# Layer 0's attention matrix: a hand-set order of all engines up to it, with an early mask, four row buffers and split square pieces

## Chip, cores and metric

One NeuronCore of a Trainium2 chip. The metric is the device time of one execution in microseconds (us). The engines are named as in the profile: PE (matmuls), DVE (VectorE), ACT (ScalarE), POOL (GpSimd), SP (issues the transfers). All times inside a run are us from the start of its span. The granted clock is the share of PE's full clock that the chip allows; a spell below 1.00 is called a throttle here.

## The reference, cut

Four graph layers act on x, shaped 32 x 512 x 128, with one 512 x 512 matrix `adj`. The change concerns what comes before layer 0's first product: layer 0 needs the softmax of a matrix `A` that is built from `adj` and a vector `e`, its diagonal apart. Layer 1 needs `adj` and a polynomial of it (here `cheb`, twice adj squared less the identity).

```python
    def _L0_gnn_ref(input, adj, W, e, bias):
        NEG = -9000000000000000.0
        h0 = jnp.einsum('bnf,fg->bng', input, W[0])
        h1 = jnp.einsum('bnf,fg->bng', input, W[1])
        m = adj > 0
        idx = jnp.cumsum(m.reshape(-1).astype(jnp.int32)) - 1
        vals = e[0][idx].reshape(adj.shape)
        A = jnp.where(m, vals, jnp.float32(NEG))
        A = jax.nn.softmax(A, axis=1)
        M = jnp.eye(adj.shape[0], dtype=A.dtype)
        out = jnp.einsum('ij,bjg->big', A * M, h0) + jnp.einsum('ij,bjg->big', A * (1.0 - M), h1)
        return out + bias[None, None, :]
    ...
    h = jnp.maximum(_layernorm(x, axis=-1), 0.0)
    x = x + _L0_gnn_ref(h, adj, L0_gnn_W, L0_gnn_e, L0_gnn_bias)
    # layers 1, 2, 3 likewise, with other bodies
```

## The kernel before

The 32 batches go in 16 pairs. `adj` lies in four blocks of 128 rows (NT = 4). A part of the program, from the masks to the attention matrix, is in the order of the source on PE, DVE, ACT and POOL (`manual_schedule`); what follows is ordered by an automatic scheduler, which may also pull an operation forward into the hand-ordered part. An engine works through its own list in order, and this is what the case is about: in b_mask below, ACT stands idle for 2.80 us before a copy, although the exponential behind it has had its input since 36.54.

```python
    def cheb_rows(i):                       # one square piece: 4 f32 matmuls (8 records in the profile), 3.43 us of PE
        p = bank(f"p_cheb_{i}")
        for t in range(NT):
            nc.tensor.matmul(p, adjT[:, t, blk(i)], adj_s[:, t, :], start=(t == 0), stop=(t == NT - 1))
        nc.scalar.mul(cheb[:, i, :], p, 2.0)
        nc.gpsimd.tensor_sub(cheb[:, i, blk(i)], cheb[:, i, blk(i)], ident)
    # ... masks m, prefix counts, one-hot rows (at_row, at_col); cheb_rows(0), cheb_rows(1)
    def softmax_rows(t):
        ph, pv = scores[t]
        none = prep.tile([P, N], F32, tag="none", name=f"none_{t}", bufs=2)
        nc.gpsimd.tensor_scalar(none, m[:, t, :], -1.0, -NEG, OP.add, OP.mult)      # the mask
        u = prep.tile([P, N], F32, tag="u", name=f"u_{t}", bufs=2)                  # a row buffer
        nc.vector.scalar_tensor_tensor(u, ph, elastn, none, OP.mult, OP.add)
        nc.vector.tensor_add(u, pv, u)
        nc.vector.tensor_reduce(least[:, t : t + 1], u, axis=AX.X, op=OP.min)
        nc.scalar.activation(u, u, AF.Exp, bias=least[:, t : t + 1], scale=-1.0,
                             accum_out=total[:, t : t + 1])
        return u

    def scaled_rows(t, u):
        nc.vector.reciprocal(total[:, t : t + 1], total[:, t : t + 1])
        nc.scalar.mul(split(att[:, t, :]), crossed(u), total[:, t : t + 1])
        nc.vector.scalar_tensor_tensor(diag[:, t, :], u[:, blk(t)], total[:, t : t + 1], ident, OP.mult, OP.mult)
        own = split(att[:, t, :])[:, :, t, :]
        nc.vector.tensor_sub(own, own, diag[:, t, :].rearrange("p (b c) -> p b c", c=QR))

    score_rows(0)
    score_rows(1)
    u = softmax_rows(0)
    cheb_rows(2)
    score_rows(2)
    for t in range(1, NT):
        un = softmax_rows(t)
        scaled_rows(t - 1, u)
        u = un
        if t == 1:
            score_rows(3)
            next(first[1])                  # transposes of pair 1
            cheb_rows(3)
    scaled_rows(NT - 1, u)
    attT = square_tile("attT")
    transpose_square(att, attT, "attT")     # 16 transposes on PE, 4 copies
    for _ in sum_steps(attT, "att", nc.vector):
        pass
    # ... adiag; projection of pair 1; then layer 0, in automatic order
```

## Time and profile before

| | kernel before |
|---|---|
| median of the first three runs | 1012.33 us |
| span of the profiled run | 1010.4 us |
| PE busy | 974.9 us |
| PE idle | 35.5 us |
| start of layer 0's first product | 59.17 us |
| start of layer 1's first product | 219.8 us |

A profile line of a timeline gives start, duration, engine, source line, operation, the tile written and the tiles read, the count, and in square brackets how long the engine stood idle just before and what ended that. The lines that carry the argument are in the prediction.

### The profile page before, as it was taken

How to read it: one execution, taken by the hardware profiler on the slowest of the kernel's cores; microseconds unless marked ns; L12 is line 12 of the kernel's file. 1: busy time of each engine (PE TensorE's matmuls, PEld its weight loads, DVE VectorE, ACT ScalarE, POOL GpSimd, SP SyncE). 2: the span in 40 equal slices, each digit the busy share in tenths (PEclk: the TensorE clock that was granted, in tenths of full speed). 3: DMA queues.
4: the chain of work that ended last, by engine and by line, in shares of the span. 5: the costliest groups of instructions: out<-in, count | busy, mean ns of one | idle time of the engine just before them, and what ended most of it. 6: DMA issues, size and time to landing. Idle time of an engine off the chain costs nothing.

```text
span 1010.4 us, 16117 instructions
## 1 busy us (share of the span) xinstructions
PE 974.9 (96%) x5918; PEld 808.2 (80%) x5918; DVE 631.5 (63%) x1526; ACT 443.1 (44%) x968; POOL 390.6 (39%) x470
## 2 busy tenths in 40 slices
PE   7698999999999999999999999999999999999997
PEld 4298999999999999998877777778667677777775
DVE  7477887755656565556846888777764544444443
ACT  4474445413223232326656433333565544444553
POOL 1258998762124421315555322221133222233332
PEclk9899999999999999999989999999999999999999
DMA  9136644511312122123434333323232112121111
GB/s 250 47 110 171 178 121 133 147 52 55 84 42 67 60 64 63 47 79 91 118 84 114 116 103 103 95 77 85 63 85 73 53 55 72 53 73 43 53 33 42
DMA packets 83007, 87.17 MB, mean 86 GB/s; under 512 B 6768, under 2 KB 73072, under 8 KB 82928
## 3 DMA queue, kind: packets, MB, share of 16 engines
q1 hardware_dynamic: 82928, 86.14, 30.4%
q8 instruction: 47, 0.77, 0.3%
q14 instruction: 32, 0.26, 0.1%
HBM read 44.70 MB, written 41.42 MB: 85 GB/s over the span
## 4 chain that ended last, share of the span: by engine, by line
PE 89%; DVE 6%; ACT 2%; DMA 1%; issue 1%; POOL 1%; SPq 0%; POOLq 0%; DVEq 0%; ACTq 0%
PE p_av L713 11%; PE p_score L701 10%; PE p_l L343 10%; PE p_msgT_c L290 4%; PE p_x1T_c L290 4%; PE p_x2T_c L290 4%; PE p_l_c L297 4%; PE p_hv L343 3%; PE p_msgT_a L290 3%; PE p_x1T_a L290 3%; PE p_x2T_d L290 3%; PE p_x2T_a L290 3%; PE p_x1T_d L290 3%; PE p_qkh L688 3%; PE p_msgT_d L290 2%; PE p_g L343 2%
## 5 line engine op out<-in xcount | busy, mean ns | idle before, releaser
L209 ACT ACTIVATE h<-x,sh,rs 128x128 f32<-128x128 f32 x384 | 154.4, 482 | 61.1 <-PE p_x2T_d L290 45.5
L706 POOL TENSOR_TENSOR ex<-ex,adjTx 128x512 f32<-128x512 f32 x64 | 83.3, 1304 | 200.2 <-issue 147.7
L702 ACT ACTIVATE ex<-p_score 128x512 f32<-128x512 f32 x128 | 71.8, 587 | 130.8 <-issue 113.0
L713 PEld LDWEIGHTS p_av<-qkh_hv,ex 128*128 128x128 f32 x1024 | 118.7, 191 | 11.5 <-issue 6.9
L713 PE MATMUL p_av<-qkh_hv,ex 128*128 128x129 f32 x1024 | 121.2, 275 | 2.2 <-POOL ex L706 1.4
L701 PE MATMUL p_score<-qkh_hv,hT 128*128 128x512 f32 x256 | 115.2, 593 | 0.0
L236 DVE STREAM_TRANSPOSE hb_hT<-h 128x512 f32<-128x512 f32 x122 | 84.7, 700 | 24.6 <-ACT h L209 23.7
L190 DVE BATCH_NORM_STATS2 bn<-x 128x6 f32<-128x256 f32 x256 | 95.4, 421 | 2.0
L706 DVE TENSOR_TENSOR ex<-ex,adjTx 128x512 f32<-128x512 f32 x64 | 45.9, 717 | 75.7 <-ACT ex L704 75.7
L701 PEld LDWEIGHTS p_score<-qkh_hv,hT 128*128 128x128 f32 x256 | 46.3, 191 | 46.4 <-issue 44.4
L704 ACT ACTIVATE ex<-ex 128x512 f32<-128x512 f32 x128 | 76.5, 630 | 1.8
L268 POOL TENSOR_TENSOR rt_h<-h 128x256 f32<-128x256 f32 x16 | 11.6, 727 | 133.9 <-PE p_x2T_c L290 133.1
L268 POOL TENSOR_TENSOR rt_feat<-feat,feat 128x256 f32<-128x256 f32 x16 | 11.6, 726 | 126.4 <-ACT feat L660 126.4
L666 POOL TENSOR_TENSOR x<-x,phi2b 128x1024 f32<-128x1024 f32 x16 | 38.0, 2377 | 33.2 <-ACT h L209 33.2
L343 PE MATMUL p_l<-th,x1T 128*128 128x128 f32 x256 | 49.5, 275 | 0.0
L343 PE MATMUL p_l<-th,x2T 128*128 128x128 f32 x256 | 49.5, 275 | 0.0
L343 PE MATMUL p_l<-th,hs 128*128 128x128 f32 x256 | 49.5, 275 | 0.0
L343 PEld LDWEIGHTS p_hv<-vw,hT 128*128 128x128 f32 x256 | 33.6, 192 | 14.9 <-issue 7.9
L369 ACT COPY g<-p_g 128x512 f32<-128x512 f32 x32 | 18.3, 579 | 61.3 <-PE p_g L343 56.2
L570 POOL TENSOR_TENSOR hd<-hT,adiag 128x512 f32<-128x512 f32 x32 | 40.4, 1274 | 3.7 <-PE p_l_e L591 2.5
L673 ACT ACTIVATE h1T<-p_phi,phi1b 128x512 f32<-128x512 f32 x32 | 21.9, 685 | 44.9 <-PE p_phi L672 44.9
L343 PEld LDWEIGHTS p_l<-th,hs 128*128 128x128 f32 x256 | 40.1, 192 | 0.8
(223 smaller groups left out, 2179.6 us busy)
## 6 DMA issues: line engine op xcount, KB each, us to landing
d_hT<-hb_hT SPq DMA_DIRECT2D x244, 128.0 KB
hT<-d_hT SPq DMA_DIRECT2D x61, 512.0 KB
x<-in_x_dram SPq DMA_DIRECT2D x32, 256.0 KB
out_dram<-x SPq DMA_DIRECT2D x32, 256.0 KB
adj_s<-in_adj_dram SPq DMA_DIRECT2D x4, 256.0 KB
adjT_d<-adjT SPq DMA_DIRECT2D x1, 1024.0 KB
sq<-in_adj_dram SPq DMA_DIRECT2D x4, 256.0 KB
adjTx<-adjT_d SPq DMA_DIRECT2D x4, 256.0 KB
```

The costliest lines, as they stand in the source:

```text
L190: ins = nc.vector.bn_stats(st[:, k].rearrange("p e s -> p (e s)"), xt[q][:, b, t : t + 2, :].rearrange("p t f -> p f t"))
L209: nc.scalar.activation(h[:, b, t, :], xt[q][:, b, t, :], AF.Relu, bias=shift[q][:, i : i + 1], scale=scale[q][:, i : i + 1])
L236: nc.vector.transpose(hb[:, :, b].rearrange("p j t r -> p t j r"), h[:, b].rearrange("p t (j c) -> p t j c", c=QR))
L290: nc.tensor.matmul(p[:, :H], b[:, k, :], a[:, k, :], start=(first and k == 0), stop=(k == 1), skip_group_check=True)
L297: nc.tensor.matmul(p[:, i * D : (i + 1) * D], a[:, k, blk(i)], b[:, k, :], start=(first and i == 0 and k == 0), stop=(k == 1), skip_group_ ...
L343: nc.tensor.matmul(p[:, blk(t)], hT(t), w, start=(i == 0), stop=(i == len(terms) - 1))
L570: nc.gpsimd.tensor_mul(split(s), src, split(scale))
L701: nc.tensor.matmul(ps, hT[:, t, b, :], qkh, start=True, stop=True)
L702: nc.scalar.activation(ex[:, t, :], ps, AF.Tanh, scale=1.0 / (8.0 * math.sqrt(D)))
L704: nc.scalar.activation(ex[:, t, :], ex[:, t, :], AF.Exp, scale=8.0)
L706: eng.tensor_mul(ex[:, t, :], ex[:, t, :], adjTx[0][:, t, :])
L713: nc.tensor.matmul(po[:, i, : D + 1], ex[:, t, blk(i0 + i)], hv[:, t, :], start=(t == 0), stop=(t == NT - 1))
```

## The change

The intent: PE waits 10.3 us for the rows of the attention matrix. So the order of all four engines up to it is written anew. The mask is made as soon as `m` exists and put into `att` itself, all four rows have a buffer of their own, the diagonal goes from DVE to POOL, `adj` is transposed row by row, a square piece is split in halves that fit holes, pieces 2 and 3 move behind the softmax, the statistics and normalization of pairs 0 and 1 are spread over waits, and the sums for the seven-product scheme are ordered as the products use them.

```diff
+    att = square_tile("att")
+    for t in range(NT):
+        nc.gpsimd.tensor_scalar(att[:, t, :], m[:, t, :], -1.0, -NEG, OP.add, OP.mult)
+    pt = [bank(f"p_adjT_{j}") for j in range(NT)]
+    for t in range(NT):
+        transpose_rows(pt, adj_s, t)        # row t into four banks
...
     def softmax_rows(t):
         ph, pv = scores[t]
-        none = prep.tile([P, N], F32, tag="none", name=f"none_{t}", bufs=2)
-        nc.gpsimd.tensor_scalar(none, m[:, t, :], -1.0, -NEG, OP.add, OP.mult)
-        u = prep.tile([P, N], F32, tag="u", name=f"u_{t}", bufs=2)
-        nc.vector.scalar_tensor_tensor(u, ph, elastn, none, OP.mult, OP.add)
+        u = prep.tile([P, N], F32, tag="u", name=f"u_{t}", bufs=NT)
+        nc.vector.scalar_tensor_tensor(u, ph, elastn, att[:, t, :], OP.mult, OP.add)
...
-        nc.vector.scalar_tensor_tensor(diag[:, t, :], u[:, blk(t)], total[:, t : t + 1], ident, OP.mult, OP.mult)
         own = split(att[:, t, :])[:, :, t, :]
-        nc.vector.tensor_sub(own, own, diag[:, t, :].rearrange("p (b c) -> p b c", c=QR))
+        d = diag[:, t, :].rearrange("p (b c) -> p b c", c=QR)
+        nc.gpsimd.tensor_mul(d, own, ident.rearrange("p (b c) -> p b c", c=QR))
+        nc.gpsimd.tensor_sub(own, own, d)
...
+    for t in range(NT):
+        score_rows(t)
+    next(project[0])
...
+    for t in range(NT):
+        if t == NT - 1:
+            next(project[0], None)          # two copies on ACT
+        us.append(softmax_rows(t))
+        if t == 0:
+            next(ln[1], None)
+        else:
+            scaled_rows(t - 1, us[t - 1])
+        for _ in range(3):
+            next(normal[1], None)           # normalization of pair 1
+    scaled_rows(NT - 1, us[-1])
+    next(turned[1])                         # transposes of pair 1
+    for t in range(NT):
+        transpose_rows(pt, att, t)
+    next(turned[1], None)
...
+    next(project[1])
+    for q in (2, 3):
+        next(ln[q])                         # statistics of pairs 2 and 3
...                                         # copies of attT, sums, adiag
+    for i in (2, 3):
+        for _ in pieces[i]:                 # square pieces 2 and 3
+            pass
     by_source.__exit__(None, None, None)
...
-        for out, op, p, q in ((s3, OP.subtract, a11, a21), (a21, OP.add, a21, a22),
-                              (s2, OP.subtract, a21, a11), (s4, OP.subtract, a12, s2)):
+        for out, op, p, q in ((s1, OP.add, a21, a22), (s2, OP.subtract, s1, a11),
+                              (a21, OP.subtract, a11, a21), (s4, OP.subtract, a12, s2)):
```

More of the change, by code (lines that the diff above doesn't have):

```diff
@@ L184, in ln_stats, with stats_steps @@
     def ln_stats(q, hold=False):
+        for _ in stats_steps(q, hold):
+            pass
+    def stats_steps(q, hold=False):
         st = stats.tile([P, NT, 2, 3], F32, tag="bn", name=f"bn_{q}", bufs=4)
@@ L193, in ln_stats @@
                 tc.keep_in_program_order(ins)
+        yield
         sd = stats.tile([P, NT, 2], F32, tag="sd", name=f"sd_{q}", bufs=4)
         nc.scalar.activation(sd, st[:, :, :, 2], AF.Sqrt, bias=eps, scale=1.0 / D)
+        yield
         rs = stats.tile([P, NT, 2], F32, tag="rs", name=f"rs_{q}")
@@ L201, in ln_stats, with normed_tile, normed_steps @@
         scale[q] = rs.rearrange("p k e -> p (k e)")
-    def normed(q, on_act=True):
-        h = work.tile([P, 2, NT, D], F32, tag="h", name=f"h_{q}", bufs=3)
+    def normed_tile(q):
+        return work.tile([P, 2, NT, D], F32, tag="h", name=f"h_{q}", bufs=3)
+    def normed_steps(q, h):
         for b in range(2):
@@ L207, in normed @@
                 i = b * NT + t
-                if on_act:
-                    nc.scalar.activation(h[:, b, t, :], xt[q][:, b, t, :], AF.Relu,
-                                         bias=shift[q][:, i : i + 1], scale=scale[q][:, i : i + 1])
-                else:
-                    nc.vector.tensor_scalar(h[:, b, t, :], xt[q][:, b, t, :], scale[q][:, i : i + 1],
-                                            shift[q][:, i : i + 1], OP.mult, OP.add)
-            if not on_act:
-                nc.scalar.activation(h[:, b], h[:, b], AF.Relu)
+                nc.scalar.activation(h[:, b, t, :], xt[q][:, b, t, :], AF.Relu,
+                                     bias=shift[q][:, i : i + 1], scale=scale[q][:, i : i + 1])
+                yield
+    def normed(q, on_act=True):
+        h = normed_tile(q)
+        if on_act:
+            for _ in normed_steps(q, h):
+                pass
+            return h
+        for b in range(2):
+            for t in range(NT):
+                i = b * NT + t
+                nc.vector.tensor_scalar(h[:, b, t, :], xt[q][:, b, t, :], scale[q][:, i : i + 1],
+                                        shift[q][:, i : i + 1], OP.mult, OP.add)
+            nc.scalar.activation(h[:, b], h[:, b], AF.Relu)
         return h
@@ L223, in transposed_by_pe, with pe_steps @@
         hT = feature_major(name)
+        for _ in pe_steps(h, name, hT):
+            pass
+        return hT
+    def pe_steps(h, name, hT):
+        ps = [bank(f"p_{name}_{b}") for b in range(2)]
         for b in range(2):
-            p = bank(f"p_{name}_{b}")
             for t in range(NT):
-                nc.tensor.transpose(p[:, blk(t)], h[:, b, t, :], ident)
+                nc.tensor.transpose(ps[b][:, blk(t)], h[:, b, t, :], ident)
+        yield
+        for b, p in enumerate(ps):
             nc.scalar.copy(hT[:, :, b, :].rearrange("p b (a c) -> p b a c", c=QR), crossed(p))
-        return hT
     def transposed(h, name):
@@ L256, in sum_steps @@
         extra = const.tile([P, 3, 2, H], F32, tag="sums", name=f"sums_{name}", bufs=3)
-        s2, s3, s4 = extra[:, 0], extra[:, 1], extra[:, 2]
-        sums[name] = {1: a11, 2: a12, 3: s4, 4: a22, 5: a21, 6: s2, 7: s3}
-        for out, op, p, q in ((s3, OP.subtract, a11, a21), (a21, OP.add, a21, a22),
-                              (s2, OP.subtract, a21, a11), (s4, OP.subtract, a12, s2)):
+        s1, s2, s4 = extra[:, 0], extra[:, 1], extra[:, 2]
+        sums[name] = {1: a11, 2: a12, 3: s4, 4: a22, 5: s1, 6: s2, 7: a21}
+        for out, op, p, q in ((s1, OP.add, a21, a22), (s2, OP.subtract, s1, a11),
+                              (a21, OP.subtract, a11, a21), (s4, OP.subtract, a12, s2)):
             tc.keep_in_program_order(eng.tensor_tensor(out, p, q, op))
@@ L357, in layer0_first @@
     def layer0_first(q):
-        ln_stats(q, hold=q in (2, 3, 4))
-        yield
+        if q >= 4:
+            ln_stats(q)
+            yield
         h = normed(q)
@@ L365, in layer0_first, with project_steps, transpose_rows @@
             yield
+        for _ in project_steps(q, hT):
+            pass
+    def project_steps(q, hT):
         g = pair_tile(f"g_{q}").rearrange("p (t b f) -> p t b f", t=NT, b=2)
+        pg = [projected(f"p_g_{q}_{b}", (at(hT, b), w0[:, 1, :])) for b in range(2)]
+        yield
         for b in range(2):
-            pg = projected(f"p_g_{q}_{b}", (at(hT, b), w0[:, 1, :]))
-            nc.scalar.copy(g[:, :, b, :], pg)
+            nc.scalar.copy(g[:, :, b, :], pg[b])
         early[q] = hT, g
-    def transpose_square(src, dst, name):
+    def transpose_rows(banks, src, t):
         for j in range(NT):
-            p = bank(f"p_{name}_{j}")
-            for i in range(NT):
-                nc.tensor.transpose(p[:, blk(i)], src[:, i, blk(j)], ident)
-            nc.scalar.copy(dst[:, j, :], p)
+            nc.tensor.transpose(banks[j][:, blk(t)], src[:, t, blk(j)], ident)
     adjT = prep.tile([P, NT, N], F32, name="adjT")
@@ L385, in cheb_rows @@
         for t in range(NT):
+            if t == 2:
+                yield
             nc.tensor.matmul(p, adjT[:, t, blk(i)], adj_s[:, t, :], start=(t == 0), stop=(t == NT - 1))
+        yield
         nc.scalar.mul(cheb[:, i, :], p, 2.0)
         nc.gpsimd.tensor_sub(cheb[:, i, blk(i)], cheb[:, i, blk(i)], ident)
-    first = {q: layer0_first(q) for q in range(NQ)}
+    first = {q: layer0_first(q) for q in range(2, NQ)}
     m = prep.tile([P, NT, N], F16, name="m")
@@ L402 @@
     nc.vector.tensor_copy(rch, rc)
-    transpose_square(adj_s, adjT, "adjT")
+    att = square_tile("att")
[4 more added lines that the diff above has]
+        transpose_rows(pt, adj_s, t)
+    for j in range(NT):
+        nc.scalar.copy(adjT[:, j, :], pt[j])
     adjT_d = bounce.tile([N, N], F32, tag="adjT", name="adjT_d", bufs=1)
@@ L415 @@
                          start=(t == 0), stop=(t == NT - 1))
-    next(first[0])
-    next(first[0])
     incl = prep.tile([P, NT], F32, name="incl")
@@ L423 @@
     nc.vector.tensor_scalar(befh, before, float(NE), None, OP.min)
-    cheb_rows(0)
+    pieces = [cheb_rows(i) for i in range(NT)]
+    next(pieces[0])
     of_row = prep.tile([P, NT, NE], F16, name="of_row")
@@ L439 @@
                              start=(t == 0), stop=(t == NT - 1))
-    next(first[0])
+    next(pieces[0])
     row_of = prep.tile([P, NK], F32, name="row_of")
@@ L456 @@
                                 accum_out=row_of[:, kk : kk + 1])
+    ln = [stats_steps(q) for q in range(4)]
+    next(ln[0])
+    next(ln[0])
     bk = prep.tile([P, NK], F32, name="bk")
@@ L464 @@
                                 accum_out=col_of[:, kk : kk + 1])
+        next(ln[0], None)
+    h = {q: normed_tile(q) for q in range(2)}
+    hT = {q: feature_major(f"hT0_{q}") for q in range(2)}
+    normal = [normed_steps(q, h[q]) for q in range(2)]
+    turned = [pe_steps(h[q], f"hT0_{q}", hT[q]) for q in range(2)]
+    project = [project_steps(q, hT[q]) for q in range(2)]
+    next(pieces[0], None)
+    for _ in normal[0]:
+        pass
+    next(pieces[1])
+    next(pieces[1])
+    next(pieces[1], None)
+    next(turned[0])
+    next(turned[0], None)
+    p = bank("p_qk_t")
+    nc.tensor.transpose(p[:, blk(0)], qw, ident)
+    nc.tensor.transpose(p[:, blk(1)], kw, ident)
+    qkT = prep.tile([P, 2, D], F32, name="qkT")
+    nc.scalar.copy(qkT, tiles(p)[:, :2, :])
     for kk in range(NK):
@@ L471 @@
                                 ecoln[:, kk : kk + 1], OP.is_equal, OP.mult)
-    cheb_rows(1)
-    next(first[0], None)
-    rights = {0: right_of(0)}
-    next(first[1])
-    next(first[1])
-    att = square_tile("att")
+    next(ln[1])
+    next(ln[1])
+    nc.scalar.activation(prep.tile([P, 1], F32, name="powers"), eps, AF.Exp)
     diag = prep.tile([P, NT, P], F32, name="diag")
@@ L509, in scaled_rows @@
         nc.scalar.mul(split(att[:, t, :]), crossed(u), total[:, t : t + 1])
-        nc.vector.scalar_tensor_tensor(diag[:, t, :], u[:, blk(t)], total[:, t : t + 1], ident, OP.mult, OP.mult)
         own = split(att[:, t, :])[:, :, t, :]
-        nc.vector.tensor_sub(own, own, diag[:, t, :].rearrange("p (b c) -> p b c", c=QR))
-    score_rows(0)
-    score_rows(1)
-    u = softmax_rows(0)
-    cheb_rows(2)
-    score_rows(2)
-    for t in range(1, NT):
-        un = softmax_rows(t)
-        scaled_rows(t - 1, u)
-        u = un
-        if t == 1:
-            score_rows(3)
-            next(first[1])
-            cheb_rows(3)
-    scaled_rows(NT - 1, u)
-    attT = square_tile("attT")
-    transpose_square(att, attT, "attT")
+        d = diag[:, t, :].rearrange("p (b c) -> p b c", c=QR)
[4 more added lines that the diff above has]
+    next(project[0])
+    p = bank("p_qk")
+    nc.tensor.matmul(p[:, :D], qkT[:, 0, :], qkT[:, 1, :], start=True, stop=True)
+    qk = const.tile([P, D], F32, name="qk")
+    attT = square_tile("attT")
+    pt = [bank(f"p_attT_{j}") for j in range(NT)]
+    us = []
+    for t in range(NT):
[10 more added lines that the diff above has]
+    next(turned[1])
+    for t in range(NT):
+        transpose_rows(pt, att, t)
+    next(turned[1], None)
+    nc.scalar.copy(qk, p[:, :D])
+    rights = {0: right_of(0)}
+    next(project[1])
+    for q in (2, 3):
+        next(ln[q])
+    for j in range(NT):
+        (nc.vector.tensor_copy if j % 2 else nc.scalar.copy)(attT[:, j, :], pt[j])
+    next(project[1], None)
     for _ in sum_steps(attT, "att", nc.vector):
@@ L538 @@
     nc.scalar.copy(adiag, p)
-    next(first[1], None)
+    for q in (2, 3):
+        next(ln[q])
+        next(ln[q], None)
+    for i in (2, 3):
+        for _ in pieces[i]:
+            pass
     by_source.__exit__(None, None, None)
@@ L544 @@
     nc.gpsimd.tensor_add(th12, th[:, 1:3, :], th[:, 3:5, :])
-    p = bank("p_qk_t")
-    nc.tensor.transpose(p[:, blk(0)], qw, ident)
-    nc.tensor.transpose(p[:, blk(1)], kw, ident)
-    qkT = prep.tile([P, 2, D], F32, name="qkT")
-    nc.scalar.copy(qkT, tiles(p)[:, :2, :])
-    p = bank("p_qk")
-    nc.tensor.matmul(p[:, :D], qkT[:, 0, :], qkT[:, 1, :], start=True, stop=True)
-    qk = const.tile([P, D], F32, name="qk")
-    nc.scalar.copy(qk, p[:, :D])
     prep_scope.close()
@@ L740, in late_sums @@
             yield from sum_steps(mat, name)
-    for q, steps in ((2, 2), (3, 2), (4, 1)):
-        for _ in range(steps):
-            next(first[q])
     waiting = [[layer0(q)] for q in range(NQ)]
+    next(waiting[0][0])
     for q in range(NQ // 2, NQ):
@@ L748 @@
     for q in range(2, NQ):
-        waiting[max(q - 4, 1)].append(first[q])
+        waiting[max(q - 4, 0)].append(first[q])
     waiting[3].append(late_sums())
```

## The prediction

> **What bounds the kernel now.** I read the page of the kernel before first: the busy shares, the forty slices, then PE's waits, then PE's and GpSimd's timelines of the first 60 us. All times are us from the span's start.
>
> ```profile
> PE 974.9 (96%) x5918; PEld 808.2 (80%) x5918; DVE 631.5 (63%) x1526; ACT 443.1 (44%) x968; POOL 390.6 (39%) x470
> ...
> PE   7698999999999999999999999999999999999997
> ...
> PEclk9899999999999999999989999999999999999999
> ```
>
> PE is busy for 974.9 of the 1010.4 us span, so all of its idle time together is 35.5 us. A change that removes no matmul can gain this, plus what a slow clock costs, and no more. The slices put the loss at the front: the first reads 7, the second 6. PE's list of waits names the parts:
>
> ```profile
> PE p_attT L376 <- DVE att L512: 10.3, 3, 6.0
> PE p_adjT L376 <- DMA adj_s<-in_adj_dram: 5.9, 4, 3.7
> PE p_l_c L297 <- DVE u_l L603: 3.5, 2, 2.7
> PE p_msgT_a L290 <- ACT feat L660: 3.5, 1, 3.5
> ...
> PE p_g L343 <- DMA hT<-d_hT: 1.2, 1, 1.2
> PE p_qk L552 <- ACT qkT L550: 0.7, 1, 0.7
> ```
>
> The largest is the wait of the transposes of the attention matrix, three times, 10.3 us. PE's timeline shows it; the columns are start, duration, work, count, and idle time before it:
>
> ```profile
> 36.89 3.60 PE L386 MATMUL p_cheb<-adj_s,adjT 128*128 128x512 f32 x8
> 40.33 0.27 PE L376 MATMUL p_attT<-ident,att 128*128 128x128 f32 x1
> 46.57 0.47 PE L376 MATMUL p_attT<-ident,att 128*128 128x128 f32 x1 [5.96 <-DVE att L512]
> 50.59 0.48 PE L376 MATMUL p_attT<-ident,att 128*128 128x128 f32 x1 [3.55 <-DVE att L512]
> 51.80 3.04 PE L376 MATMUL p_attT<-ident,att 128*128 128x128 f32 x13 [0.74 <-DVE att L512]
> ...
> 59.17 1.06 PE L297 MATMUL p_l_a<-g,attT 128*128 128x128 f32 x8
> ```
>
> Why are the rows late? VectorE waits 9.5 us in three waits for the mask `none`, and GpSimd, in order, has that mask behind the diagonal of a square piece that PE finished late:
>
> ```profile
> 33.15 0.45 POOL L388 TENSOR_TENSOR cheb<-cheb,ident 128x128 f32<-128x128 f32 x1 [2.90 <-ACT cheb L387]
> 33.67 0.62 POOL L498 TENSOR_SCALAR none<-m 128x512 f32<-128x512 f16 x1
> 41.21 0.45 POOL L388 TENSOR_TENSOR cheb<-cheb,ident 128x128 f32<-128x128 f32 x1 [6.92 <-ACT cheb L387]
> 41.74 1.31 POOL L498 TENSOR_SCALAR none<-m 128x512 f32<-128x512 f16 x2
> ```
>
> So PE's filler work (the last square piece) holds up the very chain it should cover. The first product of layer 0 starts at 59.17. From 88 to about 500 PE is nearly unbroken, and the change touches nothing there except the order of three sums.
>
> **What the Trainium skill says.** "TensorE: Matmul & The Clock Gate", Part 1, says the array runs at half clock after about 3.4 us idle and needs about 3.4 us of activity to recover. The trace agrees: the granted clock is 1.00 until 44, 0.81 in 44 to 46, 0.50 until 55, 0.75 in 55 to 56. The thirteen transposes at 51.80 take 3.04/13 = 0.234 us each, the eight of h at 17.0 take 0.94/8 = 0.117. Part 4 of the same page says transposes do not count as busy for the gate; the recovery at about 55.5, 3.7 us after a burst that is mostly transposes, speaks against that. "ScalarE: Activation LUTs", What ACT_TABLE_LOAD costs, gives 1283 ns for a load; the trace has three at 1283. "GPSIMD Engine Reference", Engine selection, says two-input elementwise work is about twice as slow there as on VectorE; here 0.454 against 0.292 us at 128x128, and 1.27 against 0.69 at 128x512.
>
> **The change part by part.** I play the new order through with the durations of this trace.
>
> 1. Transposes of adj row by row. Before, the first bank waits for all four rows and thirteen of sixteen transposes come after 7.32. Now only row 3's four do: 7.53 + 4 x 0.234 = 8.4 instead of 10.35. PE idle shrinks 5.9 to 4.8. p_incl needs `rch` (VectorE, 8.2), so it starts at 8.4, 1.9 earlier.
>
> 2. Pair 0's statistics. Before, VectorE did 1.6 of statistics at 8.19, waited 1.42 for the square root, and read p_incl at 11.53. Now it reads p_incl at about 8.75. The short operations 0.45, four mask rows at 0.72 = 2.9, two small ones 0.13, two counts 1.35: 13.6. Then the statistics 1.4: 15.0; two scans with their counts 2.1 each and the two small normalization steps 0.35: 19.7; the comparisons 1.05 in f16, 1.7 in f32: 22.4 (before 24.2); statistics of pair 1, 1.4: 23.9.
>
> 3. PE meanwhile: p_incl and p_count to 10.1, a half piece 1.7, p_row and p_before 1.9 to 13.7, other half 1.7, piece 1 3.43: 18.8. h of pair 0 comes from ScalarE at 0.40 per tile from 17.7, last at 20.9, so its transposes end at 21.0 with some 1.3 of idle; two transposes 0.23; then four scores at 2.37 (0.43+0.21+1.72): 21.2 to 30.7. Projection of pair 0 1.78 and p_qk 0.4: 32.9.
>
> 4. Softmax rows. The mask is written into `att` before 9, so the 9.5 us disappear. A row costs VectorE 2.27 (29.48 to 31.75): first 23.9 to 26.1, normalization of pair 1 0.35, then 28.7, 31.1, 33.4. Four u buffers remove the only other brake. ScalarE puts 8 x 0.40 of pair 1 and the two copies of g0 (1.1) between the exponentials; I take the copies as standing ahead of exp 3, which then ends at 35.5 instead of 34.3. Its scaling ends at 36.8 after that of row 2. GpSimd does the diagonal, 2 x 0.46 per row: rows ready at about 31, 34, 37.1, 38.0 (before 38.4 to 51.8). That part is dearer on GpSimd but frees VectorE of 4 x 0.64.
>
> 5. PE again: transposes of pair 1 to 33.8, att rows 0 and 1 to 34.8, idle about 2.3 and 0.4, rows 2 and 3 at the warm rate 0.47 each, to 38.5. Projection 1.78 and adiag 0.9 to 41.2, then square pieces 2 and 3, 6.9: 48 to 50 with handovers. I take 49.5. The copies of attT (38.6 to 40) and the four sums (4 x 0.72, to 43.2) lie under those pieces, so the sum reordering (second product after two sums, not three) saves nothing here. The Exp load is hidden (24 to 25.5), the Sqrt load too (after 42).
>
> The product starts at 49.5 instead of 59.17: **9.7 us**. The check by idle time: 16.9 before (5.9 + 10.3 + 0.7), about 8.8 after (4.8 + 1.3 + 2.7), is 8.1, and 1.9 for the slow burst at 51.8 that goes (13 x 0.117 and a part of adiag), less some 0.3 for p_count falling wholly into the slow start: 9.7.
>
> 6. After that, PE waits 1.2 at 78.5 for pair 3's transposed data and 2.7 at 84.4 for a VectorE sum that stands behind pair 5's transposes. ScalarE's h of pair 2 began at 61.99, 2.8 after the first product; now its statistics are ready at 44.8, 5 before it. The 1.2 should go. The 2.7 is an order of the queue and may survive; I count half. Together **2.5 us**.
>
> Sum: 9.7 + 2.5 = 12.2, and 1012.3 - 12.2 = **1000.1**, say 1000.0.
>
> **The rivals.** A: the wait moves. ScalarE gets 16 normalizations, copies and exponentials in one fixed order, and if rows arrive later than I have them, or the two holes at 34.8 and 37.6 with the sparse transposes throttle PE again, 2 to 4 us come back: about 1004. For it: [...]exp 3 stands behind two copies. Against: it is busy only about half of 20 to 40. B: the lead is lost in layer 0. From 90 to 200 GpSimd is busy 9.5 to 9.8 of each 10 us beside a full PE, so if layer 0 were really paced by GpSimd, a head start for PE would turn into waits. Against: GpSimd idles from 43 to 58.6 before, so its own start moves forward as well, and PE waits there only 0.8 from 120 to 300. It would leave about 6 us, 1006. C: the better start also removes the whole 3.9 and a little at the seam of layers 1 and 2 (3.5 and 1.5), because the automatic order after the hand-written part is worked out anew: about 996. It can equally make a seam worse by 2 or 3. D: a whole new loss, statistics of later pairs pulled by the scheduler into the hand-written part with a Sqrt table load between exponentials (1.28 each way). GpSimd operations were pulled in that way before (L582 at 16.13), ScalarE ones were not.
>
> **Range and chances.** To be over 2% faster it must fall below 992.5, nearly 20 us; the front holds 9.7 + 3.9 and about 5 more only at the seams. I give that 0.03. To be over 2% slower needs a collapse: 0.01. The 80% range is from C, 996.0, to between A and B, 1004.5.
>
> **What would show the steps right or wrong.** VectorE's waits for the mask gone; row sums spaced about 2.3 us; transposes of att finished near 38.5 and at 0.12 us each, granted clock 1.00 from 40 to 60; first product of layer 0 near 49.5; PE's total idle near 25; the wait for hT at the first bounced pair gone. The prediction fails if a square piece or copy again stands in front of a softmax row, if PE's idle returns between 60 and 90, or if busy time of PE grows with a second throttling.

## The result, and the profile after

The changed kernel took 999.78 us in the median (996.94 to 1000.45, four runs) against 1012.88 (1012.07 to 1015.63, four runs) beside it. The ratio is 0.9861, 95% interval 0.9833 to 0.9888: 1.4% faster. All ratios here are the mean time of one kernel's fast runs over the mean of the other's fast runs of the same rounds, so not quite the ratio of the medians.

The page of the kernel after, the busy shares and PE's row of the slices:

```profile
PE 976.4 (98%) x5918; PEld 809.4 (81%) x5918; DVE 630.4 (63%) x1520; ACT 440.9 (44%) x967; POOL 395.1 (40%) x478
...
PE   8999999999999999999899999999999999999997
```

The span is 998.5, so PE's idle time is 998.5 - 976.4 = 22.1 us (35.5 before), and the first two slices are 8 and 9 instead of 7 and 6. PE's waits, in the same list as before (total, times, longest):

```profile
PE p_adjT L403 <- DMA adj_s<-in_adj_dram: 4.2, 2, 3.4
PE p_msgT_a L312 <- ACT feat L724: 3.5, 1, 3.5
PE p_attT L403 <- ACT hT L251: 2.1, 1, 2.1
...
PE p_l_c L319 <- DVE u_l L667: 1.4, 3, 0.8
```

The wait of the attention transposes went from 10.3 to 2.1 (and 0.3 more in a line not shown). The list puts the 2.1 down to ACT's copy of hT. Row 2 of the matrix, which is transposed next, left POOL at 36.04 + 0.45 = 36.49, just before PE goes on at 36.54, so the row is the likelier cause. The wait for pair 3's bounced data (transposed by way of a transfer) is not in the list any more; the one for the VectorE sum fell from 3.5 to 1.4 (2.0 in the second profile below). The 3.5 at the seam to layer 2 stayed to the tenth. PE's timeline:

```profile
33.37 1.07 PE L403 MATMUL p_attT<-ident,att 128*128 128x128 f32 x8
36.54 0.66 PE L403 MATMUL p_attT<-ident,att 128*128 128x128 f32 x4 [2.10 <-ACT hT L251]
37.49 0.66 PE L403 MATMUL p_attT<-ident,att 128*128 128x128 f32 x4 [0.29 <-POOL att L566]
37.98 3.25 PE L365 MATMUL p_g<-w,hT 128*128 128x128 f32 x16
...
42.29 7.03 PE L414 MATMUL p_cheb<-adj_s,adjT 128*128 128x512 f32 x16
49.16 1.05 PE L319 MATMUL p_l_a<-g,attT 128*128 128x128 f32 x8
```

The first product of layer 0 starts at 49.16 instead of 59.17, layer 1 at 206.4 instead of 219.8. Two things are to be seen. The hole of 2.10 is where the prediction put "about 2.3". And the sixteen matmuls of the projection at 37.98 take 3.25 where the sixteen of pair 0 at 30.39 took 1.95. Here is the throttle that the prediction named among its rivals. A second profile of the same kernel (the run `after_again` below) has the same hole without it:

```profile
37.43 0.66 PE L403 MATMUL p_attT<-ident,att 128*128 128x128 f32 x4 [0.29 <-POOL att L566]
37.93 1.95 PE L365 MATMUL p_g<-w,hT 128*128 128x128 f32 x16
...
40.61 7.03 PE L414 MATMUL p_cheb<-adj_s,adjT 128*128 128x512 f32 x16
47.48 1.06 PE L319 MATMUL p_l_a<-g,attT 128*128 128x128 f32 x8
```

Granted clock of the two profiles in windows of 2 us (columns: window, its length, PE busy with count, granted clock, DMA share, GB/s), first the profile, then the second one:

```profile
38.00:40.00 2.00, 2.00 (x14) 0.60 0.09 6
40.00:42.00 2.00, 2.00 (x12) 0.55 0.19 68
```

```profile
38.00:40.00 2.00, 2.00 (x20) 1.00 0.04 5
40.00:42.00 2.00, 2.00 (x11) 1.00 0.22 69
```

From 30 to 37.5 the two agree within 0.1 us, then one runs at half clock for 3.4 us, and its first product is 49.16 - 47.48 = 1.7 us later. At layer 1's first product 206.40 - 205.26 = 1.1 of it is left. The spans differ by 2.2 (998.5 and 996.3). The other 1.1 comes at the seam to layer 2, where the profile on record shows half clock from about 492.4 to 499.2 and the second one only from about 493.2 to 496.6.

Of eight timed runs of this kernel, the three with a mean granted clock of 0.996 took 996.94, 997.20 and 998.04, the five with 0.993 or 0.994 took 999.23 to 1000.45. The means are 997.4 and 999.8: the kernel after has two levels 2.4 us apart, and the same program gets either. The mean clock adds up all spells of a run, and only two of the eight were profiled, so the spell at 38 is shown for one run, as about half of the difference.

A third spell lies at the end. PE's last twenty matmuls in the kernel before, and then in the kernel after:

```profile
1003.70 2.50 PE L713 MATMUL p_av<-qkh_hv,ex 128*128 128x129 f32 x20 [0.42 <-POOL ex L706]
```

```profile
990.20 4.14 PE L777 MATMUL p_av<-qkh_hv,ex 128*128 128x129 f32 x20 [0.42 <-POOL ex L770]
```

The kernel after is 219.81 - 206.40 = 13.4 us ahead at layer 1 and still 13.5 ahead here. It then loses 4.14 - 2.50 = 1.6 to the clock (granted 0.50 in 992 to 994, against 1.00 in 1004 to 1006 before), which leaves the 11.9 between the spans. This does not go with the change: of the fourteen profiles, before, b_mask_u4, a_stats, a_fill and a_fill_sums have 2.50, the other nine have 4.14.

### The profile page after: what moved, and what is told of

The parts are those of the page before. It is cut to its first block, busy times and chain, and to the rows that moved or that the text cites. A ratio compares the mean times of both kernels' runs of the same rounds, so it can differ in the third digit from the quotient of the medians.

```text
span 998.5 us, 16127 instructions
## 1 busy us (share of the span) xinstructions
PE 976.4 (98%) x5918; PEld 809.4 (81%) x5918; DVE 630.4 (63%) x1520; ACT 440.9 (44%) x967; POOL 395.1 (40%) x478
## 3 DMA queue, kind: packets, MB, share of 16 engines
q1 hardware_dynamic: 82928, 86.14, 30.7%
## 4 chain that ended last, share of the span: by engine, by line
PE 88%; DVE 6%; ACT 2%; DMA 1%; issue 1%; POOL 1%; SPq 1%; POOLq 0%; DVEq 0%; ACTq 0%
PE p_av L777 11%; PE p_score L765 10%; PE p_l L365 10%; PE p_msgT_c L312 4%; PE p_l_c L319 4%; PE p_x1T_c L312 4%; PE p_x2T_c L312 4%; PE p_hv L365 3%; PE p_g L365 3%; PE p_msgT_a L312 3%; PE p_x1T_a L312 3%; PE p_x1T_d L312 3%; PE p_x2T_a L312 3%; PE p_x2T_d L312 3%; PE p_qkh L752 3%; PE p_l_d L319 3%
## 5 line engine op out<-in xcount | busy, mean ns | idle before, releaser
L730 POOL TENSOR_TENSOR x<-x,phi2b 128x1024 f32<-128x1024 f32 x16 | 38.0, 2375 | 33.2 <-ACT h L216 33.2
L365 PE MATMUL p_l<-th,x2T 128*128 128x128 f32 x256 | 49.5, 275 | 0.0
L365 PE MATMUL p_l<-th,x1T 128*128 128x128 f32 x256 | 49.5, 275 | 0.0
L365 PE MATMUL p_l<-th,hs 128*128 128x128 f32 x256 | 49.5, 275 | 0.0
L737 ACT ACTIVATE h1T<-p_phi,phi1b 128x512 f32<-128x512 f32 x32 | 21.9, 686 | 44.9 <-PE p_phi L736 44.9
```

The costliest lines, as they stand in the source:

```text
L365: nc.tensor.matmul(p[:, blk(t)], hT(t), w, start=(i == 0), stop=(i == len(terms) - 1))
```

## The experiments

Because the clock and the arrival of `adj` vary from run to run (the start of the mask of the last block of `adj` on DVE lies between 5.8 and 7.5 us), the timed ratios separate only effects above some 2 us. I therefore read two distances from the profiles, each free of the arrival: **R**, from the start of the mask of adj's last block on DVE to the end of the last transpose of the attention matrix (rows ready), and **L**, from layer 0's first product to layer 1's first product (what PE loses in the ramp, the first 40 us or so after that product, and in the rest of layer 0). Two profiles of the kernel after give R = 31.32 and 31.27, and L = 157.2 and 157.8. R also counts as a gain that square pieces 2 and 3 (7 us of PE) move from in front of the last transpose to behind it. From the same mask to layer 0's first product, where they are counted in every kernel, it is 51.88 before, 46.70 in b_three, and 42.33 and 40.66 in the two profiles after. Each other row is one profile, so I read nothing into differences below 0.7.

| run | what it is | median us | ratio to before, 95% interval | R | L |
|---|---|---|---|---|---|
| before | | 1012.33 | 1 | 47.55 | 160.6 |
| after | | 999.78 | 0.9861 (0.9833 to 0.9888) | 31.32 | 157.2 |
| after_again | the same | 998.65 | 0.9862 (0.9845 to 0.9879) | 31.27 | 157.8 |
| b_mask | before + early mask | 1009.70 | 0.9969 (0.9941 to 0.9997) | 44.30 | 162.0 |
| b_mask_u4 | + four row buffers | 1008.29 | 0.9954 (0.9935 to 0.9972) | 43.67 | 160.6 |
| b_three | + diagonal on POOL | 1007.81 | 0.9950 (0.9928 to 0.9971) | 42.52 | 160.6 |
| a_latemask | after, mask late | 1008.52 | 0.9958 (0.9942 to 0.9973) | 39.87 | 157.3 |
| a_u2 | after, two row buffers | 1001.42 | 0.9888 (0.9867 to 0.9910) | 33.69 | 157.1 |
| a_diag | after, diagonal on DVE | 1001.32 | 0.9887 (0.9866 to 0.9907) | 33.69 | 156.8 |
| a_jmajor | after, adj transposed bank by bank | 1000.00 | 0.9865 (0.9846 to 0.9884) | 33.38 | 157.7 |
| a_sums | after, old order of sums | 997.57 | 0.9842 (0.9822 to 0.9862) | 30.99 | 157.6 |
| a_stats | after, statistics of pairs 2 to 4 late | 998.33 | 0.9853 (0.9827 to 0.9879) | 31.58 | 157.9 |
| a_fill | after, square piece 2 in the hole | 997.62 | 0.9853 (0.9836 to 0.9869) | 31.61 | 160.5 |
| a_fill_sums | a_fill, late sums later | 996.85 | 0.9836 (0.9815 to 0.9857) | 31.96 | 160.0 |

All outputs are right. Kernels are compared only within the same rounds. So compare ratios. My theory was that PE waited for one chain of in-order handovers (mask on POOL, row on DVE, exponential and scaling on ACT, diagonal on DVE), and that the change gains by taking foreign work out of that chain's way. The rival was that one part, the mask, is the change.

### after_again: the kernel after once more

No edit.

> The changed kernel unaltered, as the measure for the other runs of this call. Expected 997 to 1001 us. Theory: its spread comes from whether PE's clock is throttled a second time around 38 to 42 us (in the profiled run the granted clock was 0.50 there for 3.4 us and the 16 projection matmuls took 3.05 us instead of 1.78); runs with a mean granted clock of 0.996 should be near 997, with 0.993 near 1000.

Measured: 998.65 us, 997.20 to 999.65, with the clock levels told above. The two levels are as expected. That the throttle at 38 makes them is half shown: between the two profiles it accounts for 1.1 of 2.2 us, and the spell at the seam to layer 2 for the rest.

### b_mask: the early mask alone, in the kernel before

```diff
     nc.vector.tensor_copy(rch, rc)
+    att = square_tile("att")
+    for t in range(NT):
+        nc.gpsimd.tensor_scalar(att[:, t, :], m[:, t, :], -1.0, -NEG, OP.add, OP.mult)
...
-        none = ...; nc.gpsimd.tensor_scalar(none, m[:, t, :], -1.0, -NEG, OP.add, OP.mult)
-        nc.vector.scalar_tensor_tensor(u, ph, elastn, none, OP.mult, OP.add)
+        nc.vector.scalar_tensor_tensor(u, ph, elastn, att[:, t, :], OP.mult, OP.add)
```

> The kernel before with the early mask alone: the mask is written into att right after m, everything else as before. Theory 'the order': VectorE's 9.5 us of waits for the mask go, but ScalarE still has exp 2 behind the copy of the last square piece (40.5 in the kernel before) and row 3 still waits for a row buffer of two; worked out on the trace of before, exp 2 ends at 41.9, row 1 is scaled at 42.5, row 3 ends on VectorE at 44.8 and is scaled at 46.4, against 51.75: gain about 5 us, time about 1007.5. Rival 'the mask is the change': nearly the whole 10 us, time about 1002. Third: nothing, PE waits for other things, 1012.

Measured: 0.9969, R shorter by 3.25 of the 16.2 us that the whole change takes off. The mask waits are gone and other ones have come. ACT's timeline of this run:

```profile
40.61 0.60 ACT L387 ACTIVATE cheb<-p_cheb 128x512 f32<-128x512 f32 x1 [2.80 <-PE p_cheb L386]
41.10 0.71 ACT L503 ACTIVATE u<-u,least 128x512 f32<-128x512 f32 x1
```

and DVE's:

```profile
42.55 0.29 DVE L512 TENSOR_TENSOR att<-att,diag 128x128 f32<-128x128 f32 x1 [5.56 <-ACT att L509]
42.76 0.75 DVE L500 SCALAR_TENSOR_TENSOR u<-p_first,elastn,att 128x512 f32<-128x512 f32 x1
```

The copy of the last square piece stands on ACT ahead of exponential 2, so ACT waits for PE to finish that filler. Exponential 2 delays the scaling of row 1, DVE's subtraction for row 1 waits 5.56 us for that scaling, and row 3 stands behind the subtraction. The order, as worked out beforehand, is right; the gain was expected at 5 us and is about 3. "The mask is the change" falls.

### b_mask_u4 and b_three: buffers, then the diagonal

```diff
-        u = prep.tile([P, N], F32, tag="u", name=f"u_{t}", bufs=2)
+        u = prep.tile([P, N], F32, tag="u", name=f"u_{t}", bufs=NT)      # b_mask_u4
...
-        nc.vector.scalar_tensor_tensor(diag[:, t, :], ...); nc.vector.tensor_sub(own, own, diag ...)
+        nc.gpsimd.tensor_mul(d, own, ident ...); nc.gpsimd.tensor_sub(own, own, d)   # b_three
```

> The kernel before with early mask and four row buffers, the diagonal still on VectorE. Theory: no gain over the mask alone, because VectorE's subtraction for row 1 waits for ScalarE in front of row 3 whatever the buffers: VectorE's row 3 again starts at about 42.8 and the first product at about 55.9; time 1008 to 1011. Rival: the buffers were what held row 3: row 3 at about 37, first product near 53.

> The kernel before with three parts of the change: early mask, four row buffers, diagonal on GpSimd; engine orders otherwise as before. In the run with the mask alone VectorE's subtraction for row 1 waited 5.6 us for a scaling that stood on ScalarE behind the copy of the last square piece, and row 3 stood behind it. Theory: rows 2 and 3 now run on VectorE without a wait (done by about 36), but exponential 2 still waits for that copy (40.6), then exponentials and scalings follow back to back: last row ready at about 45.4 instead of 48.1, first product near 53 (mask alone: 55.9), time about 1006.5. What then still lies between it and the changed kernel (about 998.7) is the order itself. Rival: the three parts do it all, about 1001.

Measured with four buffers: DVE again waits 5.47 us for the scaling of row 1 before row 3, and R shortens by 0.6. Counted from the mask of adj's last block, the copy of the last square piece on ACT is already 0.56 us earlier in this run, before a buffer could matter. So the buffers give nothing there. With the diagonal on POOL as well, DVE has finished all rows by 37.7, and R is 42.5. What is left stands on ACT:

```profile
40.57 0.60 ACT L387 ACTIVATE cheb<-p_cheb 128x512 f32<-128x512 f32 x1 [2.80 <-PE p_cheb L386]
41.07 0.71 ACT L503 ACTIVATE u<-u,least 128x512 f32<-128x512 f32 x1
```

Three parts together take 5.0 of 16.2 us off R. With them in place, 42.52 - 31.3 = 11.2 us are left to the order itself and to the row-by-row transposes of `adj`; but up to the first product the parts take 51.88 - 46.70 = 5.2 of 51.88 - 40.66 = 11.2, and only 6.0 are left, because R leaves out the two pieces that the order moves. Of the rivals, "the three parts do it all" falls.

### a_latemask: the mask late again, in the kernel after

```diff
-    for t in range(NT):
-        nc.gpsimd.tensor_scalar(att[:, t, :], m[:, t, :], -1.0, -NEG, OP.add, OP.mult)
...
     def softmax_rows(t):
         ph, pv = scores[t]
+        nc.gpsimd.tensor_scalar(att[:, t, :], m[:, t, :], -1.0, -NEG, OP.add, OP.mult)
```

> The changed kernel with the mask late again: each row's mask is made on GpSimd just ahead of the row's softmax, in att itself. Theory: masks 2 and 3 now stand behind the diagonal work of rows 0 and 1 on GpSimd, which waits for the scaling; row 2 starts on VectorE at about 33.2 instead of 28.4 and row 3 at about 38.6 instead of 30.7; first product of layer 0 about 6 us later (55 instead of 49.2), time 1004 to 1007. Rival, mask only mattered because of the square pieces' diagonals in front of it, which the new order has moved away: no more than 1.5 us (row 0), about 1001.

Measured: 0.9958, so some 70% of the gain is lost; the first product comes at 57.5. POOL's timeline:

```profile
33.12 0.45 POOL L565 TENSOR_TENSOR att<-att,diag 128x128 f32<-128x128 f32 x1
33.66 0.62 POOL L550 TENSOR_SCALAR att<-m 128x512 f32<-128x512 f16 x1
...
39.19 0.62 POOL L550 TENSOR_SCALAR att<-m 128x512 f32<-128x512 f16 x1
```

Masks 2 and 3 stand behind the diagonal work of rows 0 and 1, as expected. DVE waits 3.19 and 3.20 us for them; row 2 starts at 34.31 and row 3 at 39.84 (33.2 and 38.6 were worked out; 28.43 and 30.66 in the kernel after). The size was short: 6 us expected, 8.4 measured in the first product, because row 3 starts 9.2 late where 7.9 was worked out, and the longer holes go with a throttle (granted clock 0.80 in 30 to 40 and 0.52 in 40 to 50). How much is hidden behind ACT's copies was not tested. The same mask that is worth 3 us in the old order is worth 8.5 in the new one, both read from R.

### a_u2 and a_diag: buffers and diagonal undone one at a time

```diff
-        u = prep.tile([P, N], F32, tag="u", name=f"u_{t}", bufs=NT)
+        u = prep.tile([P, N], F32, tag="u", name=f"u_{t}", bufs=2)        # a_u2
...
-        nc.gpsimd.tensor_mul(d, own, ident ...); nc.gpsimd.tensor_sub(own, own, d)
+        nc.vector.scalar_tensor_tensor(diag[:, t, :], ...); nc.vector.tensor_sub(own, own, diag ...)   # a_diag
```

> The changed kernel with two row buffers instead of four. Theory: row 2 may start only when row 0 is scaled (29.9 in the profile after, it started at 28.43) and row 3 when row 1 is scaled; worked through, exp 3 ends about 1.9 us later, so the first product of layer 0 comes 1.5 to 2 us later (49 to 49.5 against 47.5 without the second throttle). Time about 1000.5. Rival: no difference, because exp 3 stands behind two copies on ScalarE anyway: 998.7.

> The changed kernel with the diagonal back on VectorE. Theory: the subtraction stands in VectorE's order ahead of the next row and waits for ScalarE's scaling, so rows 2 and 3 start about 1.8 and 3.7 us later (30.2 and 34.4 against 28.4 and 30.7); the last row then is ready about 1.6 us later although VectorE's own two operations are shorter than GpSimd's: first product at about 49, time about 1000.3. Rival, the operations' durations decide (0.64 us per row on VectorE against 0.91 on GpSimd): no loss, 998.7.

Measured: both 0.989, both R = 33.69, 2.4 us longer. DVE's timeline with two buffers:

```profile
29.05 0.75 DVE L553 SCALAR_TENSOR_TENSOR u<-p_first,elastn,att 128x512 f32<-128x512 f32 x1 [1.48 <-issue]
...
32.93 0.75 DVE L553 SCALAR_TENSOR_TENSOR u<-p_first,elastn,att 128x512 f32<-128x512 f32 x1 [1.54 <-issue]
```

The profile names no releaser here ("issue"), but ACT's scaling of row 0 ends at 28.97 and that of row 1 at 32.85, and each row starts 0.08 us after: the buffer was the wait. DVE's timeline with the diagonal on it:

```profile
30.23 0.29 DVE L565 TENSOR_TENSOR att<-att,diag 128x128 f32<-128x128 f32 x1 [1.03 <-ACT att L562]
...
34.19 0.29 DVE L565 TENSOR_TENSOR att<-att,diag 128x128 f32<-128x128 f32 x1 [1.04 <-ACT att L562]
```

The two subtractions wait about 1.03 each for ACT and hold rows 2 and 3 back. DVE needs 0.292 us for what takes POOL 0.456, and it is still the wrong engine, as what costs is the place in the queue. The delays were expected at 1.9 and 1.6 us, so short by 0.5 and 0.8. Either part alone leaves row 2 waiting for the scaling of row 0, so each is needed for the other to pay. Both undone at once was not run.

### a_jmajor: adj transposed bank by bank

```diff
-    for t in range(NT):
-        transpose_rows(pt, adj_s, t)
     for j in range(NT):
+        for i in range(NT):
+            nc.tensor.transpose(pt[j][:, blk(i)], adj_s[:, i, blk(j)], ident)
         nc.scalar.copy(adjT[:, j, :], pt[j])
```

> The changed kernel with adj transposed bank by bank again. Theory: thirteen of the sixteen transposes wait for the last row of adj and run at half clock, so the count of the prefix sums and all of VectorE's chain starts about 1.9 us later, and the first product with it: about 49.4 instead of 47.5, time about 1000.5. Rival: PE has later holes that take it up (about 1.3 before the scores, 2.1 before row 2), so under 0.7 us.

Measured: 0.9865, no difference in the timed runs. In the profile R is 33.38, 2.1 us longer, and the prefix counts start 2.85 after the mask of adj's last block instead of 0.95 and 1.06. But in that run the last block came 0.9 us earlier, and the two nearly cancel in its first product (49.70). The chain's 1.9 us are shown; that they reach the time is not, the interval being 2 us either way.

### a_sums: the old order of the sums

```diff
-        for out, op, p, q in ((s1, OP.add, a21, a22), (s2, OP.subtract, s1, a11),
-                              (a21, OP.subtract, a11, a21), (s4, OP.subtract, a12, s2)):
+        for out, op, p, q in ((s3, OP.subtract, a11, a21), (a21, OP.add, a21, a22),
+                              (s2, OP.subtract, a21, a11), (s4, OP.subtract, a12, s2)):
```

> The changed kernel with the old order of the sums. Theory (step 5 of the prediction): the sums lie under the last two square pieces and later sums are far ahead of their use: no difference, within 1 us of 998.7, first product and the three after it without a new wait. Rival: the second product waits 0.7 us somewhere, up to 1 us slower.

Measured: 0.9842, R and L as in the kernel after. There is no new wait. The reordering is worth nothing here, as the sums lie under 6.9 us of square pieces. Its PE timeline is worth a look for another reason:

```profile
3.35 3.68 PE L403 MATMUL p_adjT<-ident,adj_s 128*128 128x128 f32 x16 [3.35 <-DMA adj_s<-in_adj_dram]
...
7.14 1.02 PE L451 MATMUL p_count<-upto,rch 128*128 128x512 f16 x4
8.00 1.88 PE L414 MATMUL p_cheb<-adj_s,adjT 128*128 128x512 f32 x4
```

In this run the rows of `adj` came close together, so PE did nothing but transposes from 3.35 to 6.85 (and ten matmuls of one column). The four count matmuls at 7.14 then start every (8.00 - 7.14)/4 = 0.215 us, the full rate; in the kernel after, whose transposes were broken by a wait, the same four needed (9.87 - 8.21)/4 = 0.415. Transposes alone had released the clock here. They do not do so every time: in a_u2 they ran as unbroken, from 3.70 to 7.17, and the counts behind them still came every (9.12 - 7.46)/4 = 0.415 us. The view of the granted clock reads 1.00 through all of this, in all three runs, so the slow start is to be seen in the spacing alone.

### a_stats: statistics of pairs 2 to 4 late again

```diff
-    for q in (2, 3):
-        next(ln[q])
...
-        if q >= 4:
-            ln_stats(q)
-            yield
+        ln_stats(q, hold=q in (2, 3, 4))
+        yield
...
+    for q, steps in ((2, 2), (3, 2), (4, 1)):
+        for _ in range(steps):
+            next(first[q])
...
-        waiting[max(q - 4, 0)].append(first[q])
+        waiting[max(q - 4, 1)].append(first[q])
```

> The changed kernel with the statistics of pairs 2, 3 and 4 handled as before, after the hand-written part. First product of layer 0 unchanged or a little earlier (VectorE has 2.7 us less before the copies of attT). Theory: normalization of pairs 2 and 3 starts several us later, and PE waits again between the first product and 30 us after it, 2 to 4 us (before: 1.2 for transposed data and 2.7 for a VectorE sum): time 1001 to 1002. Rival: the lead does not matter, 998.7.

Measured: 0.9853, L = 157.9, and PE waits 1.4 us in all between 45 and 100. My expectation missed: with the statistics early PE waits as much there, 0.8 and 1.4 us in the two profiles of the kernel after, so the lead does not hang on their place. ACT starts the normalization of pair 2 at 46.7 in this run, still 2.7 us before the first product at 49.4 (before: 2.8 after it). I put the room down to square pieces 2 and 3, 6.9 us of PE work that asks nothing of DVE and now lies between the attention matrix and the first product; a_fill tests this.

### a_fill and a_fill_sums: can the hole be used?

```diff
     for t in range(NT):
+        if t == 2:
+            next(pieces[2])
+            next(pieces[2])
         transpose_rows(pt, att, t)
...
-    waiting[3].append(late_sums())
+    waiting[6].append(late_sums())          # a_fill_sums only
```

> The changed kernel with square piece 2 moved from the end of the hand-written part into the hole between the transposes of att rows 1 and 2, where PE idled 2.1 us. Theory 'the hole costs its idle time and a throttle': idle gone (2.1) and clock stays 1.00 from 38 to 42 (1.6): first product of layer 0 at about 45.5 instead of 49.2, time about 996, and the spread of the timed runs smaller. Rival 'given back': sums, diagonal and pair 2's data are then not ready and PE waits in 45 to 70 instead: 998 to 1000.

> The changed kernel with square piece 2 in the hole and GpSimd's sums of adj and cheb started three pairs later. In the run with the hole filled, the first product came 3.4 us earlier but two thirds were lost again by 90 us: PE waited 1.6 for a VectorE sum that stood behind GpSimd's additions, one of the late sums among them, and 0.8 for pair 3's bounced data. Theory: without the late sums in the ramp the 1.6 goes: about 996 (hole filled alone: 997.6). Rival: the ramp is bound by the bounced transposes and the wait only moves: 997.6.

Measured with the hole filled: the hole is gone, the clock stays at 1.00, the first product comes at 44.05, 3.4 us before that of `after_again`; yet the ratio is 0.9853 and L is 160.5, as in the kernel before. PE's timeline in the ramp:

```profile
64.51 2.02 PE L365 MATMUL p_g<-w,hT 128*128 128x128 f32 x16 [0.82 <-DMA hT<-d_hT]
...
81.18 1.16 PE L319 MATMUL p_l_c<-rt_g,attT 128*128 128x128 f32 x8 [1.64 <-DVE u_l L670]
```

The idle time reappears as a wait for pair 3's transposed data, which goes through a transfer, and as a wait for the VectorE sum: the two waits of the kernel before, 1.2 and 2.7, are back as 0.8 and 1.6. With the late sums moved, PE's timeline has this:

```profile
66.14 2.02 PE L365 MATMUL p_g<-w,hT 128*128 128x128 f32 x16 [2.78 <-DMA hT<-d_hT]
```

The 1.6 goes and the 0.8 becomes 2.8. The rival of both expectations was right. From the mask of adj's last block to layer 1's first product it is 198.4 us in `after_again`, 198.1 in `a_fill` and 197.9 in `a_fill_sums`. So a better version is not shown; a_fill_sums has the lowest median (996.85), with an interval that overlaps the kernel after, and its profile has neither the throttle at 38 nor the half clock at the end. These two runs say what a_stats only suggested: moving one square piece away from the ramp brings the old waits back, although the statistics stay early. ACT then starts the normalization of pair 2 at 43.84, only 0.2 us before the first product.

## Why the prediction was right

**Time.** 1000.0 predicted, 999.78 measured, well inside 996.0 to 1004.5. The sum was right in part by luck: one term had the wrong cause, one hid another, and one was not in it. At layer 1 the kernel after is 13.4 us ahead, where 12.2 was predicted for the whole; the 1.6 us of half clock at the very end, which no step foresaw, brings the spans back to 11.9 apart.

**Steps 1 to 5, the chain.** In the profile the prefix counts started at 7.89 (8.4 predicted), DVE read them at 8.38 (8.75), the comparisons ended at 21.9 (22.4), the scores ran from 20.94 to 30.4 (21.2 to 30.7), the last row left DVE at 32.9 (33.4), its exponential ended at 34.8 (35.5), the last rows were ready at 36.5 and 37.4 (37.1 and 38.0). All are early by about the half microsecond by which the last block of `adj` came earlier. The hole measured 2.10 (2.3) and 0.29 (0.4). The experiments confirm the mechanism part by part (late mask, buffers, diagonal, transposes by row), with the sizes short in a_latemask.

**First product.** 49.16 against 49.5, but partly by luck. The steps came to 48.1 and I added 1.4 for handovers. Without a throttle it starts at 47.48, so there is hardly any such cost. What filled the place of it in the profile on record is the throttle of 1.7 us that I had listed as rival A and expected not to see: "granted clock 1.00 from 40 to 60" failed in this profile and held in the second. PE's busy time, a sign of failure that the prediction named, grew from 974.9 to 976.4 in the one and not in the other (973.9).

**Step 6, the ramp.** 2.5 us expected, L shortened by 2.8 to 3.4. The size holds, and so does the lead: ACT starts the normalization of pair 2 2.8 us after the first product in the kernel before, 3.9 and 3.3 ahead of it in the two profiles after, and only 0.2 ahead in a_fill, where the waits are back. What fails is what gives the lead: the prediction named the early statistics ("now its statistics are ready at 44.8, 5 before it"). a_stats makes them late again; the lead is still 2.7 and L does not move. The place of square pieces 2 and 3 gives it: a_fill takes one of them away and L returns to 160.5.

**Rivals.** A (throttle) happened in one of the two profiles, at 1.7 us in the first product and 1.1 at layer 1; in the six runs without a profile it stays open which spells made the two levels. B (GpSimd paces layer 0) did not: L got shorter. C (seams change by themselves) did not by the waits: 3.5, 1.8 and 1.5 are the same before and after; only the length of the half clock at the seam to layer 2 varies. D (a Sqrt load among the exponentials) did not. The sum reordering saves nothing, as said.

**Readings.** Two are off without harm. The 7.53 of step 1 seems to be the start at 7.32 with the 0.21 of waiting before it added on once more. And GpSimd is busy 9.4 to 9.8 of each 10 us only from 90 to 160; from there to 200 it is 7.6 to 8.3, so rival B was weaker than it was made out.

## What to carry to other kernels

Where PE waits for a chain over four in-order engines, ask at each link what stands ahead of it in the queue; the mask, the buffers and the diagonal were each worth 2 to 8 us in the order that had nothing else in the way, and together 5 in the order that had. Filler work on PE also brings its copies and corrections to the other engines, so it belongs behind the chain, and there it has a second use: it gives the next stage time to prepare. Before one fills a hole, one should ask who uses the time that the filler now covers, as here the hole could be filled and nothing measurable came of it. And a difference of 2 us between two such kernels can be spells of half clock alone (1.1, 1.1 and 1.6 us here): look for them in both profiles before explaining it.

## What the Trainium skill lacked or had wrong

- "TensorE: Matmul & The Clock Gate", Part 4, says that transposes do not count as busy in the same way and that the full clock does not engage for them. In a_sums, transposes alone (3.35 to 6.85) were followed by count matmuls at 0.215 us, the full rate; in a_u2 as long a stretch was followed by 0.415. So transposes can release the clock, and one such stretch does not always. The profile does not say in which mode they ran.
- Part 1 of the page ties the fall of the clock to an idle window of about 3.4 us; here the longest hole was 2.1 us, with 0.3 and short bursts after it, and the granted clock fell to 0.50 for 3.4 us in one of two profiles of the same kernel. This contradicts the page only if transposes count as busy: from 32.40 to 37.98 PE did nothing but transposes and waits, 5.6 us. No run here separates the two.
- "ScalarE: Activation LUTs", What ACT_TABLE_LOAD costs, adds a drain of about 1380 ns to each load. In the profile after, the load takes from 23.71 to 24.99, the activation before it ends at 23.69 and the next one starts at 25.00: no such gap is visible.
